# A pairwise bilinear kernel: weights loaded four pairs at a time, inputs one field at a time, outputs stored two pairs at a time

## The chip, the core and the metric

The kernel runs on one core of a Trainium2 chip. The metric is the device time of one execution in microseconds (us); the time before is the median of seven runs.

## What is computed

There are 32 fields of 128 numbers for each of 1024 samples, and one 128 x 128 matrix for each of the 496 pairs (i, j) of fields with i < j. Each pair gives one output block of 1024 x 128, all in float32:

```python
v_i = inputs[:, I_IDX, :]                                # (1024, 496, 128)
v_j = inputs[:, J_IDX, :]
transformed = jnp.einsum('bpd,ped->bpe', v_i, W)         # W: (496, 128, 128)
return transformed * v_j
```

The inputs are 16.8 MB, the weights 32.5 MB and the output 260 MB.

## The kernel before

Everything is laid out transposed: the 128 numbers of a field (or of an output block) lie over the 128 partitions, the 1024 samples along the free dimension. In HBM a field is 128 rows of 4 KB, and two neighbouring fields lie side by side in each partition's row. The weights lie in groups, each partition's part of a group being contiguous, and so do the output blocks.

The pairs are taken with i falling from 30 to 0 and j rising from i + 1 to 31, so the blocks of pairs with equal i grow from 1 pair to 31. A pair is worked on in two halves of 512 samples, called units; unit u is half u % 2 of pair u // 2.

*Numbers.* Only the first 15 pairs (NATIVE) are multiplied in plain float32, by one matmul (L145). For all others, x and the weights are split into a high, a low and a difference part in the format float32r. split_w (L87 to L95) does this for a chunk of four pairs (WC = 4): one operation on ScalarE (L92) and three on GpSimd (L93 to L95). split_x (L100 to L109) does it for half a field in the same way (L106, then L107 to L109). A unit then has two matmuls into a PSUM bank (L148), a scaling of that bank in place by ScalarE (L149), and a third matmul on top of it (L157). VectorE multiplies the bank by x_j and writes it into an output tile (L163).

*Order.* The order is written out by hand in one loop over units. In each step, `first(u)` issues L145, or L148 and L149; `second(u - LAG)` with LAG = 3 issues L157, L163 and, when a tile is full, its store. Splits come from a list sorted by due time. PSUM has eight banks, one unit each.

*Transfers.* All loads of weights (L83) and, but for the first two fields, of x (L74), and all stores (L167, and L165 for the halves of the last two pairs) are issued by one queue, SyncE's (SP), in the order of the program. A load of weights brings WL = 8 pairs in 4 KB rows into one of three buffers, and is issued WLEAD = 2 groups ahead. A load of x brings two fields in 8 KB rows; they stay for the whole run. An output tile holds OG = 1 pair; there are six tiles (L64), and VectorE's first write into a tile (L163) waits until the tile's last store has landed. Each DMA issued also waits until the DMA eight places before it has landed.

The lines that set how much is moved at once:

```python
t = xpool.tile([P, n, BT], F32, tag=f"x{f}", name=f"x_{f}")
w_raw[c] = rpool.tile([P, WL, P], F32, tag="w", name=f"w_{c}")
ots[g] = opool.tile([P, OG, BT], F32, tag="ot", name=f"ot_{g}")
```

Of the kernel before, what the change touches and what calls it, by code (L numbers as in the profile page):

```python
# [1 line left out]

# [4 lines left out]

F32 = mybir.dt.float32
F32R = mybir.dt.float32r
ALU = mybir.AluOpType  # L10

P = 128
NF = 32
NQ = NF * (NF - 1) // 2
BT = 1024
HB = 512
WC = 4
WL = 8
OG = 1
EPS = 2.0**-12  # L20
NATIVE = 5
LAG = 3
WLEAD = 2
XLEAD = 4


def _pairs():

    return [(i, j) for i in range(NF - 2, -1, -1) for j in range(i + 1, NF)]


@with_exitstack
def kernel(
    ctx: ExitStack,
    tc: tile.TileContext,
    xt: bass.AP,
    wt: bass.AP,
    out: bass.AP,
):

    nc = tc.nc
    pairs = _pairs()
    nchunk = NQ // WC

    xpool = ctx.enter_context(tc.tile_pool(name="x", bufs=1))  # L60
    spool = ctx.enter_context(tc.tile_pool(name="xs", bufs=2))
    rpool = ctx.enter_context(tc.tile_pool(name="wr", bufs=3))
    wpool = ctx.enter_context(tc.tile_pool(name="ws", bufs=3))
    opool = ctx.enter_context(tc.tile_pool(name="o", bufs=6))  # L64
    ppool = ctx.enter_context(tc.tile_pool(name="ps", bufs=8, space=bass.MemoryType.PSUM))

    x_sb = {}

    def load_x(f, n=1, pieces=1, eng=None):

        t = xpool.tile([P, n, BT], F32, tag=f"x{f}", name=f"x_{f}")
        s = BT // pieces
        for k in range(pieces):
            (eng or nc.sync).dma_start(out=t[:, :, k * s : (k + 1) * s], in_=xt[:, f : f + n, k * s : (k + 1) * s])  # L74
        for k in range(n):
            x_sb[f + k] = t[:, k, :]

    w_raw = {}

    def load_w(c, splits=(0, WL)):  # L80
        w_raw[c] = rpool.tile([P, WL, P], F32, tag="w", name=f"w_{c}")
        for a, b in zip(splits, splits[1:]):
            nc.sync.dma_start(out=w_raw[c][:, a:b, :], in_=wt[c, :, a:b, :])  # L83

    w_s = {}

    def split_w(c):  # L87

        k = c * WC % WL
        raw = w_raw[c * WC // WL][:, k : k + WC, :].rearrange("p q e -> p (q e)")  # L90
        h, l, d = [wpool.tile([P, WC * P], F32R, tag=t, name=f"{t}_{c}") for t in ("wh", "wl", "wd")]
        nc.scalar.mul(h, raw, 1.0 - 2.0**-13)  # L92
        nc.gpsimd.tensor_tensor(l, raw, h.bitcast(F32), ALU.subtract)  # L93
        nc.gpsimd.tensor_scalar(d, h.bitcast(F32), EPS, 1.0, ALU.mult, ALU.mult)  # L94
        nc.gpsimd.tensor_tensor(d, l.bitcast(F32), d.bitcast(F32), ALU.subtract)  # L95
        w_s[c] = (h, l, d)

    x_s = {}

    def split_x(f, a):  # L100

        if a == 0:
            x_s[f] = [spool.tile([P, BT], F32R, tag=t, name=f"{t}_{f}") for t in ("xh", "xl", "xd")]
        s = slice(a, a + HB)
        h, l, d = [t[:, s] for t in x_s[f]]
        nc.scalar.mul(h, x_sb[f][:, s], 1.0 - 2.0**-13)  # L106
        nc.gpsimd.tensor_tensor(l, x_sb[f][:, s], h.bitcast(F32), ALU.subtract)  # L107
        nc.gpsimd.tensor_scalar(l, l.bitcast(F32), 1.0 / EPS, 1.0, ALU.mult, ALU.mult)  # L108
        nc.gpsimd.tensor_tensor(d, h.bitcast(F32), l.bitcast(F32), ALU.subtract)  # L109

    nq0 = NATIVE * (NATIVE + 1) // 2
    c0 = nq0 // WC
    first_q = {i: q for q, (i, j) in reversed(list(enumerate(pairs)))}

    todo = []
    for c in range(c0, nchunk):
        todo.append(((c - 2) * WC + 1, max(c * WC, nq0), lambda c=c: split_w(c)))
    for i in range(NF - 2 - NATIVE, -1, -1):  # L120
        for a in range(0, BT, HB):
            todo.append((first_q[i + 1] + 1 if i < NF - 3 - NATIVE else 2, first_q[i], lambda i=i, a=a: split_x(i, a)))
    todo.sort(key=lambda t: t[1])

    load_w(0, (0, 1, WL))
    load_x(NF - 2, pieces=2, eng=nc.scalar)
    load_x(NF - 1, pieces=2, eng=nc.scalar)
    load_x(NF - 3)
    load_x(NF - 4)
    load_w(1)  # L130
    load_x(NF - 6, 2)


    ctx.enter_context(tc.manual_schedule())
    po, ots = {}, {}


    def first(u):
        q, h = divmod(u, 2)
        i, c = pairs[q][0], q // WC  # L140
        r = slice(q % WC * P, (q % WC + 1) * P)
        s = slice(h * HB, (h + 1) * HB)
        po[u] = ppool.tile([P, HB], F32, tag="po", name=f"po_{u}")
        if q < nq0:
            nc.tensor.matmul(po[u], w_raw[q // WL][:, q % WL, :], x_sb[i][:, s], start=True, stop=True)  # L145
        else:
            for t in (0, 1):
                nc.tensor.matmul(po[u], w_s[c][t][:, r], x_s[i][t][:, s], start=t == 0, stop=t == 1)  # L148
            nc.scalar.mul(po[u], po[u], 1.0 + EPS)  # L149

    def second(u):
        q, h = divmod(u, 2)
        i, j = pairs[q]
        r = slice(q % WC * P, (q % WC + 1) * P)
        s = slice(h * HB, (h + 1) * HB)
        if q >= nq0:
            nc.tensor.matmul(  # L157
                po[u], w_s[q // WC][2][:, r], x_s[i][2][:, s], start=False, stop=True, skip_group_check=True
            )
        g, k = divmod(q, OG)  # L160
        if k == 0 and h == 0:
            ots[g] = opool.tile([P, OG, BT], F32, tag="ot", name=f"ot_{g}")
        nc.vector.tensor_tensor(ots[g][:, k, s], po.pop(u), x_sb[j][:, s], ALU.mult)  # L163
        if q >= NQ - 2:
            nc.sync.dma_start(out=out[g, :, k, s], in_=ots[g][:, k, s])  # L165
        elif k == OG - 1 and h == 1:
            nc.sync.dma_start(out=out[g], in_=ots[g])  # L167

    for u in range(2 * NQ + LAG):
        q = u // 2  # L170
        if u % (2 * WL) == 0 and (q // WL + WLEAD) * WL < NQ:
            load_w(q // WL + WLEAD)
        if u < 2 * NQ:
            i, j = pairs[q]
            if u % 2 == 0 and j == i + 1 and i % 2 == 0 and 0 <= i - 2 - XLEAD:
                load_x(i - 2 - XLEAD, 2)
            first(u)
        if u >= LAG:
            second(u - LAG)
        if u % 2 == 1:  # L180
            ready = [t for t in todo if t[0] <= q]
            if ready:
                ready[0][2]()
                todo.remove(ready[0])
    assert not todo


# [25 lines left out]
```

## Time and profile before

| | |
|---|---|
| median of 7 runs | 781.07 us (779.4 to 787.55) |
| the profiled execution's own time | 782.89 us |
| its span in the profile | 781.1 us |
| granted TensorE clock, mean | 0.976 |
| read from HBM, written to it | 49.28 MB, 260.05 MB |
| over the span | 396 GB/s |

The span runs from the first to the last instruction that the profile shows. PE is TensorE's matmuls, PEld its weight loads, DVE is VectorE, ACT ScalarE, POOL GpSimd and SP SyncE. A group's line gives the source line, the engine and the operation, the tiles written and read, the number of instructions, the busy time and mean duration of one in ns, then the engine's idle time just before them and what ended most of it. A line of DMA issues gives the tiles, the queue, the count, the size and the median us from issue to landing. A digit in the DMA row is the mean busy share of the 16 DMA engines in a fortieth of the span, in tenths (9 is 90% or more); the DMA packet line counts packets by size, and the queue lines give packets, MB and the time that the packets took as a share of 16 engines' span. The chain of waits lists start, length and what ran.

### The profile page before, as it was taken

How to read it: one execution, taken by the hardware profiler on the slowest of the kernel's cores; microseconds unless marked ns; L12 is line 12 of the kernel's file. 1: busy time of each engine (PE TensorE's matmuls, PEld its weight loads, DVE VectorE, ACT ScalarE, POOL GpSimd, SP SyncE). 2: the span in 40 equal slices, each digit the busy share in tenths (PEclk: the TensorE clock that was granted, in tenths of full speed). 3: DMA queues.
4: the chain of work that ended last, by engine and by line, in shares of the span. 5: the costliest groups of instructions: out<-in, count | busy, mean ns of one | idle time of the engine just before them, and what ended most of it. 6: DMA issues, size and time to landing. Idle time of an engine off the chain costs nothing.

```text
span 781.1 us, 11576 instructions
## 1 busy us (share of the span) xinstructions
PE 715.8 (92%) x2946; PEld 557.9 (71%) x2946; DVE 634.9 (81%) x992; ACT 617.1 (79%) x1136; POOL 550.5 (70%) x523
## 2 busy tenths in 40 slices
PE   7989889898997998998998999899999999999994
PEld 3468668676776876776776877777777777777773
DVE  4678768787896978887896988789888889889886
ACT  1279779797886986987886888788888888888883
POOL 0998998787776885866767586767685767594550
PEclk9999999999998999999999999999999999999998
DMA  9999999999999999999999999999999999999997
GB/s 357 417 377 400 409 388 407 404 397 396 412 400 399 389 392 405 400 387 402 403 392 402 390 403 405 398 400 391 404 403 404 401 400 408 404 401 400 403 414 317
DMA packets 83730, 310.10 MB, mean 397 GB/s; under 512 B 9296, under 2 KB 9424, under 8 KB 81872
## 3 DMA queue, kind: packets, MB, share of 16 engines
q1 hardware_dynamic: 83088, 308.32, 100.4%
q10 hardware_dynamic: 576, 1.05, 0.4%
q8 instruction: 23, 0.38, 0.2%
q14 instruction: 43, 0.35, 0.1%
HBM read 49.28 MB, written 260.05 MB: 396 GB/s over the span
## 4 chain that ended last, share of the span: by engine, by line
DMA 53%; DVE 23%; PE 17%; POOL 3%; issue 1%; SPq 0%; DVEq 0%; ACT 0%; POOLq 0%
DMA out_dram<-ot 51%; DVE ot L163 23%; PE po L148 12%; PE po L157 5%; DMA x<-in_xt_dram 1%; POOL xd L109 1%; POOL xl L107 1%; DMA w<-in_wt_dram 1%; POOL wl L93 0%; POOL xl L108 0%; POOL wd L95 0%; DVEq L163 0%; SPq L83 0%; ACT xh L106 0%; POOL wd L94 0%
## 5 line engine op out<-in xcount | busy, mean ns | idle before, releaser
L163 DVE TENSOR_TENSOR ot<-po,x 128x512 f32<-128x512 f32 x992 | 634.9, 686 | 139.1 <-DMA out_dram<-ot 102.2
L149 ACT ACTIVATE po<-po 128x512 f32<-128x512 f32 x962 | 539.4, 581 | 137.1 <-PE po L148 90.4
L148 PE MATMUL po<-xh,wh 128*128 128x512 f32 x962 | 387.9, 403 | 49.0 <-DVE ot L163 48.9
L148 PE MATMUL po<-xl,wl 128*128 128x512 f32 x962 | 380.7, 396 | 2.2 <-POOL wl L93 1.7
L157 PE MATMUL po<-xd,wd 128*128 128x512 f32 x962 | 379.4, 395 | 0.0
L93 POOL TENSOR_TENSOR wl<-w,wh 128x512 fp32r<-128x512 f32 x121 | 156.2, 1291 | 158.1 <-ACT wh L92 158.1
L148 PEld LDWEIGHTS po<-xh,wh 128*128 128x128 f32 x962 | 183.4, 191 | 114.5 <-DVE ot L163 74.6
L157 PEld LDWEIGHTS po<-xd,wd 128*128 128x128 f32 x962 | 183.9, 191 | 40.3 <-ACT po L149 0.4
L148 PEld LDWEIGHTS po<-xl,wl 128*128 128x128 f32 x962 | 184.0, 191 | 37.7 <-POOL wl L93 2.1
L95 POOL TENSOR_TENSOR wd<-wl,wd 128x512 fp32r<-128x512 f32 x121 | 156.6, 1294 | 10.1
L107 POOL TENSOR_TENSOR xl<-x,xh 128x512 fp32r<-128x512 f32 x52 | 67.2, 1293 | 23.1 <-ACT xh L106 23.1
L94 POOL TENSOR_SCALAR wd<-wh 128x512 fp32r<-128x512 f32 x121 | 75.2, 622 | 10.2
L92 ACT ACTIVATE wh<-w 128x512 fp32r<-128x512 f32 x121 | 75.7, 627 | 0.0
L109 POOL TENSOR_TENSOR xd<-xh,xl 128x512 fp32r<-128x512 f32 x52 | 67.0, 1288 | 4.3
L106 ACT ACTIVATE xh<-x 128x512 fp32r<-128x512 f32 x52 | 32.6, 631 | 13.8 <-DMA x<-in_xt_dram 13.8
L108 POOL TENSOR_SCALAR xl<-xl 128x512 fp32r<-128x512 f32 x52 | 32.3, 622 | 4.6
L145 PE MATMUL po<-x,w 128*128 128x512 f32 x60 | 29.2, 651 | 4.2 <-DMA x<-in_xt_dram 4.2
L145 PEld LDWEIGHTS po<-x,w 128*128 128x128 f32 x60 | 12.1, 207 | 20.5 <-issue 13.8
L106 ACT ACT_TABLE_LOAD x1 | 1.3, 1283 | 2.6 <-issue 2.6
L200 POOL MEMSET const-float32-0.0<- 128x1 f32 x1 | 0.1, 99 | 0.2 <-issue 0.2
L200 POOL MEMSET const-bfloat16-1.0<- 128x1 bf16 x1 | 0.1, 102 | 0.0
L200 POOL MEMSET const-uint8-127<- 128x1 uint8 x1 | 0.1, 102 | 0.0
(1 smaller groups left out, 0.1 us busy)
## 6 DMA issues: line engine op xcount, KB each, us to landing
out_dram<-ot SPq DMA_DIRECT2D x494, 512.0 KB, 7.6
w<-in_wt_dram SPq DMA_DIRECT2D x61, 512.0 KB, 7.2
x<-in_xt_dram SPq DMA_DIRECT2D x14, 1024.0 KB, 10.3
x<-in_xt_dram ACTq DMA_DIRECT2D x4, 256.0 KB, 5.7
x<-in_xt_dram SPq DMA_DIRECT2D x2, 512.0 KB, 6.8
out_dram<-ot SPq DMA_DIRECT2D x4, 256.0 KB, 6.1
w<-in_wt_dram SPq DMA_DIRECT2D x1, 448.0 KB, 4.6
w<-in_wt_dram SPq DMA_DIRECT2D x1, 64.0 KB, 3.1
```

Source lines behind the costliest of these rows:

```text
L92: nc.scalar.mul(h, raw, 1.0 - 2.0**-13)
L93: nc.gpsimd.tensor_tensor(l, raw, h.bitcast(F32), ALU.subtract)
L94: nc.gpsimd.tensor_scalar(d, h.bitcast(F32), EPS, 1.0, ALU.mult, ALU.mult)
L95: nc.gpsimd.tensor_tensor(d, l.bitcast(F32), d.bitcast(F32), ALU.subtract)
L106: nc.scalar.mul(h, x_sb[f][:, s], 1.0 - 2.0**-13)
L107: nc.gpsimd.tensor_tensor(l, x_sb[f][:, s], h.bitcast(F32), ALU.subtract)
L109: nc.gpsimd.tensor_tensor(d, h.bitcast(F32), l.bitcast(F32), ALU.subtract)
L145: nc.tensor.matmul(po[u], w_raw[q // WL][:, q % WL, :], x_sb[i][:, s], start=True, stop=True)
L148: nc.tensor.matmul(po[u], w_s[c][t][:, r], x_s[i][t][:, s], start=t == 0, stop=t == 1)
L149: nc.scalar.mul(po[u], po[u], 1.0 + EPS)
L157: nc.tensor.matmul(po[u], w_s[q // WC][2][:, r], x_s[i][2][:, s], start=False, stop=True, skip_group_check=True)
L163: nc.vector.tensor_tensor(ots[g][:, k, s], po.pop(u), x_sb[j][:, s], ALU.mult)
```

## The change

WL goes from 8 to 4: a load of weights brings four pairs, in 2 KB rows instead of 4 KB, into one of five buffers instead of three, and is issued four groups ahead instead of two, so still 16 pairs. OG goes from 1 to 2: an output tile holds two pairs, a store writes 1 MB in 8 KB rows, and there are three tiles instead of six, with the same memory in all. The layout of the output and of the weights in HBM follows OG and WL. A load of x brings one field in 4 KB rows, at the start of each block of pairs with equal i, instead of two fields at every second block. Ahead of the loop, fields 27 and 26 are loaded one by one, and two more groups of weights. SP then issues 247 stores of 1 MB, 125 loads of weights and 30 loads of x, and the four stores of halves at the end as before. The order of the compute instructions stays the same on each engine.

```diff
-WL = 8
-OG = 1
+WL = 4
+OG = 2
 ...
-WLEAD = 2
-XLEAD = 4
+WLEAD = 4
+XLEAD = 3
 ...
-    rpool = ctx.enter_context(tc.tile_pool(name="wr", bufs=3))
+    rpool = ctx.enter_context(tc.tile_pool(name="wr", bufs=5))
 ...
-    opool = ctx.enter_context(tc.tile_pool(name="o", bufs=6))
+    opool = ctx.enter_context(tc.tile_pool(name="o", bufs=3))
 ...
     load_w(1)
-    load_x(NF - 6, 2)
+    for f in range(NF - 5, NF - 4 - XLEAD, -1):
+        load_x(f)
+    load_w(2)
+    load_w(3)
 ...
-            if u % 2 == 0 and j == i + 1 and i % 2 == 0 and 0 <= i - 2 - XLEAD:
-                load_x(i - 2 - XLEAD, 2)
+            if u % 2 == 0 and j == i + 1 and 0 <= i - 2 - XLEAD:
+                load_x(i - 2 - XLEAD)
```

## Prediction

> **What bounds the kernel now.** I read the page first: the engines' shares, the DMA rows, then the releasers. Next come the waits of VectorE (DVE) and the chain of work in a late stretch.
>
> ```profile
> PE 715.8 (92%) x2946; PEld 557.9 (71%) x2946; DVE 634.9 (81%) x992; ACT 617.1 (79%) x1136; POOL 550.5 (70%) x523
> DMA  9999999999999999999999999999999999999997
> DMA packets 83730, 310.10 MB, mean 397 GB/s; under 512 B 9296, under 2 KB 9424, under 8 KB 81872
> q1 hardware_dynamic: 83088, 308.32, 100.4%
> L163 DVE TENSOR_TENSOR ot<-po,x 128x512 f32<-128x512 f32 x992 | 634.9, 686 | 139.1 <-DMA out_dram<-ot 102.2
> L148 PE MATMUL po<-xh,wh 128*128 128x512 f32 x962 | 387.9, 403 | 49.0 <-DVE ot L163 48.9
> out_dram<-ot SPq DMA_DIRECT2D x494, 512.0 KB, 7.6
> w<-in_wt_dram SPq DMA_DIRECT2D x61, 512.0 KB, 7.2
> x<-in_xt_dram SPq DMA_DIRECT2D x14, 1024.0 KB, 10.3
> ```
>
> No compute engine is full: PE has most, and 48.9 us of its idle time is blamed on DVE, whose own 139.1 us of idle is mostly (102.2) waiting for a store to give an output tile back. The DMA engines are at nine tenths or more in every slice but the last, and one queue alone accounts for 100.4% of sixteen engines. So the bound is DMA time. Next, what a tile does, from the chain of waits:
>
> ```profile
> 606.70 3.88 DVE ot L163 x6
> 610.58 0.02 issue
> 610.60 7.64 DMA out_dram<-ot
> ...
> 634.15 7.42 DMA out_dram<-ot
> 641.57 0.03 issue
> 641.60 0.05 DVEq L163
> 641.65 0.04 issue
> 641.69 0.70 DVE ot L163
> ```
>
> A store issues 0.02 us after DVE's last write; 7.4 to 7.6 us later it lands; 0.12 us after that DVE starts (641.57 to 641.69). DVE's pace in a row is 3.88/6 = 0.647 us an operation.
>
> **What a packet costs.** In the trace's packet records the median durations on q1 are 84 ns (2 KB rows), 159 (4 KB), 309 (8 KB, only loads of x) and 9 (the 4-byte completion): 9 ns plus 75 ns per 2 KB. At the very end, where one DMA engine works alone, starts lie 80 ns apart for 2 KB, 155 for 4 KB and 6 for a completion, so some 4 ns of each overlap. I take 305 for 8 KB, an estimate (309 - 4). A DMA puts 8 rows and one completion on each of 16 engines: 512 KB in 4 KB rows 8 x 155 + 6 = 1.246 us, 1 MB in 8 KB rows 2.446, 256 KB in 2 KB rows 0.646.
>
> Against the whole of before: 494 stores, 62 weight loads' worth and x come to about 735 us per engine; DMA is active from 3.3 us to the end, some 775. The other 40 are stalls and instruction fetches. Packets last longer than their medians by 7.7 us (8 KB) and 24 us (4 KB) per engine.
>
> **The change part by part.**
>
> *Stores, 494 of 512 KB to 247 of 1 MB (8 KB rows):* 247 x (2 x 1.246 - 2.446) = -11.4 us. *Weights, 62 loads in 4 KB rows to 124 in 2 KB rows:* 62 x (2 x 0.646 - 1.246) = +2.9. *x, 14 loads of two fields to 28 of one, 8 KB to 4 KB rows:* 14 x 0.046 = +0.6. Together -7.9 us. Every microsecond is on the path, as the DMA engines have no gap. Upper bound of the gain: the full 9 ns per removed packet, (83088 - 58464) x 9 / 16 = -13.9 us. Lower bound: none; the last landings in the trace come 1.25 us apart for 512 KB in 4 KB rows and 0.63 apart for 256 KB in 2 KB rows, the same per byte. Below nothing it goes only if 8 KB stores stall (rival 2). I take -7.9, between.
>
> Here rules speak against the row. The Trainium skill ("DMA: Bandwidth & Descriptors", Specifications) has line rate from 512 B up, so 2, 4 and 8 KB rows would cost the same and this part is worth 0; by 80, 155 and 305 ns it is -7.9. The same page (Rules for kernel authors) asks for 1 MiB or more per DMA, and gives (Anatomy of one DMA) some 2 us fixed for each, there for DMAs issued from GpSimd: 62 more weight loads would be +124 us and 247 fewer stores -494, if DMAs ran one at a time. In this trace neither shows: behind a queued store a 512 KB weight load lands 1.24 us after it, so the fixed time is hidden by the queue. I follow the rows.
>
> *Stalls of x.* The 8 KB rows of x last 378 ns in the mean for a median of 309. Behind a queued store a 1 MB load of x lands 3.6 us later, where two stores take 2.6. The start of the run has x in 4 KB rows: excess 2 ns a packet, against 33 for the 8 KB rows right after. The 4 KB rows of weights have about 13 (stretches with a weight load have 7.3 a packet, stretches of stores alone 4.7, and a third of the packets are the load's: 4.7 + 3 x 2.6). If x takes 13 per 4 KB, 1792 x (69 - 26)/16 = -4.8 us. Bounds: 0 if the stall goes by bytes, +7.7 if by packet, -7.7 if it goes. I take -4.8, nearest to the 4 KB rows of x and w. *Stalls of weights:* 2 KB rows of x at the start have 0.6 ns excess; if by packet, 7900 more x 13/16 = +6.4; if by byte 0. I take +1.
>
> *Tiles, six of one pair to three of two.* The bytes are the same; the grain is not. Before: fill 2 x 0.647, start and issue 0.14, empty-queue latency 1.2 (the fastest first landing of a 512 KB store is 2.45 us after issue, less its 1.25), transfer 1.3: 3.9 us out of six periods of 1.55 = 9.3. So 5.4 us of queue wait are forecast, and 7.6 - 2.5 = 5.1 are there. After: fill 2.59, 0.14, 1.2, transfer 2.53: 6.46 us out of three periods of 3.1 = 9.3, leaving 2.8 us. Positive, so the slowest DMA engine still has work. But engines differ: in the trace the first of 16 completions of a store comes at 4.6 us (median) and the last at 7.6, a spread of 3. With 2.8 us of cover the fastest engines will sometimes run dry. They catch nothing up later, so I charge +2; bounds 0 (a dry fast engine isn't the bound) and +17 (rival 2).
>
> *Waits on SP.* A store now waits for four DVE writes instead of two. Queued behind it on SP are the next weight load or x; they lead by nine pairs (14 us) for weights, as before, and four or more fields for x. No one needs them that early. Each DMA waits on the one eight before it; with at most three stores out that one has landed. The first split of x needs one field at about 15.5 us instead of two at 17.7, since less is loaded ahead; DMA is saturated there anyway, so 0. Compute instructions stay the same in number and order; PE at 0.68 us a unit (0.45 + 0.23 in the chain) needs 2.72 us per two pairs, DVE 2.59: both below the 3.1 that the DMA engines need. Fewer SP instructions are worth 0.
>
> Sum: -7.9 - 4.8 + 1 + 2 = -9.7 us on the profiled execution's 782.9 us (1.8 around its 781.1 span): 773.2. That execution lies 1.8 above the median of 781.07, so 771.4 against the median.
>
> **The rivals.**
> 1. *Rows don't matter* (0.2): the wire gain is nil as the last landings suggest, and the x stall goes by bytes: 781.1 + 1 + 2 = 784, or 778 if half of both gains comes (-6.4); 781 in the middle. For it: equal landings per byte at the end. Against: the packet starts.
> 2. *Three tiles are too few* (0.3, slower). Each load of x delays some DMA engine more than the mean: a 1 MB load cost the slowest 1.0 us and the mean engine 0.55. With 5.1 us of wait the others absorb that; with 2.8 against a spread of 3.0 the loss is paid each time, and every new stall of the slowest stops all 16. Worked out: 28 loads x up to 0.6 us = +17, on top of -7.9 + 1: 791. It decides from 11.7 us of added dry time (7.9 + 4.8 - 1), that is 0.047 us per two-pair tile. Stalls of 8 KB stores would do the same: 6 ns a packet over 31616 packets / 16 engines is 11.9 us. No store of 8 KB rows is in the trace; instruction fetches of 8 KB last 309, without stalls, which speaks against it.
> 3. *Everything at its best* (part of the forecast's own side): -13.9 - 7.7 gives 760.
>
> **How the numbers follow.** The forecast case (771.4, own range 764 to 777) has 0.5, rival 1 (777 to 784) 0.2, rival 2 (785 to 800) 0.3. A measurement here tells some 0.5%, 3.9 us, from no change: faster 0.5, same 0.18, slower 0.32, a little of rival 1 spilling over. The range reaches from 763 to 793, leaving out the end of rival 2 and the best case.
>
> **What would show it.** Right: q1 with 58464 packets and 8 KB stores at a median of 309; DMA rows still at 9; store landing near 6.5 us for 1 MB (9.2 less 2.59 and 0.14); DVE's waits for stores still first; mean of x packets near 170 ns. Wrong: 8 KB packets well above 309 in the mean; DMA share falling under nine tenths in middle slices with fewer than 16 packets in flight (rival 2); PE or ACT becoming the releaser of most DVE idle; more GB/s without a shorter span can't be, as the bytes are fixed.

## The result and the profile after

The changed kernel takes 773.94 us (median of 12 runs, 769.92 to 776.26), the kernel before 781.17 us (31 runs): a ratio of 0.9902, 95% interval 0.9884 to 0.992, or -7.7 us. The forecast was -9.7 us (771.4). The profiled execution took 772.85 us against 782.89.

These are the lines of the page after that answer to those shown of before:

```profile
PE 721.7 (94%) x2946; PEld 552.8 (72%) x2946; DVE 617.2 (80%) x992; ACT 620.0 (80%) x1136; POOL 550.8 (71%) x523
DMA  9899999999999999999999999999999999999999
DMA packets 59102, 310.04 MB, mean 402 GB/s; under 512 B 6561, under 2 KB 6817, under 8 KB 27425
q1 hardware_dynamic: 58464, 308.31, 99.4%
L166 DVE TENSOR_TENSOR ot<-po,x 128x512 f32<-128x512 f32 x992 | 617.2, 684 | 147.9 <-DMA out_dram<-ot 92.5
L151 PE MATMUL po<-xh,wh 128*128 128x512 f32 x962 | 390.7, 406 | 37.0 <-DVE ot L166 34.8
out_dram<-ot SPq DMA_DIRECT2D x247, 1024.0 KB, 6.2
w<-in_wt_dram SPq DMA_DIRECT2D x123, 256.0 KB, 5.9
x<-in_xt_dram SPq DMA_DIRECT2D x30, 512.0 KB, 7.3
```

The bytes are the same, the packets some 30% fewer, and the queue still fills its engines to 99.4%. The DMA row has an 8 in its second slice, where before it had a 9. A 1 MB store lands 6.2 us after its issue (6.5 was forecast). DVE's main wait is still for a store.

The packet records tell more, as us for each of the 16 engines. "Stalls" is what all packets of q1 last beyond 9 ns and 75 ns per 2 KB; "dry" is the time with fewer than 16 packets in flight between 45 and 750 us, counted as missing packets over 16.

| | before | after |
|---|---|---|
| packets of q1 | 83088 | 58464 |
| stalls, us | 31.7 | 28.0 |
| of them 8 KB packets | 7.7 (x) | 23.0 (stores) |
| dry, us | 3.0 | 4.7 |
| first to last completion of a store, median us | 3.05 | 1.48 |

With the prediction's 5 ns for a packet, 24624 packets fewer are worth -7.7 us; with -3.7 for stalls and +1.7 for dry time that makes -9.7, and the two profiled executions differ by -10.0. So the sum looks as forecast. But the experiments show that its term for the tiles was far too small, and that two others were off the other way and made up for it.

### The profile page after: what moved, and what is told of

Its sections match the earlier page's. It is cut to its first block, busy times and chain, and to the rows that moved or that the text cites. A ratio compares the mean times of both kernels' runs of the same rounds, so it can differ in the third digit from the quotient of the medians.

```text
span 771.1 us, 10983 instructions
## 1 busy us (share of the span) xinstructions
PE 721.7 (94%) x2946; PEld 552.8 (72%) x2946; DVE 617.2 (80%) x992; ACT 620.0 (80%) x1136; POOL 550.8 (71%) x523
## 3 DMA queue, kind: packets, MB, share of 16 engines
q1 hardware_dynamic: 58464, 308.31, 99.4%
## 4 chain that ended last, share of the span: by engine, by line
DMA 42%; PE 33%; DVE 22%; issue 1%; DVEq 0%; SPq 0%; ACTq 0%
DMA out_dram<-ot 41%; DVE ot L166 22%; PE po L151 22%; PE po L160 10%; DMA x<-in_xt_dram 1%; DVEq L166 0%; ACTq L74 0%; SPq L74 0%; SPq L83 0%; DVEq L209 0%; SPq L170 0%
## 5 line engine op out<-in xcount | busy, mean ns | idle before, releaser
L166 DVE TENSOR_TENSOR ot<-po,x 128x512 f32<-128x512 f32 x992 | 617.2, 684 | 147.9 <-DMA out_dram<-ot 92.5
L94 POOL TENSOR_SCALAR wd<-wh 128x512 fp32r<-128x512 f32 x121 | 75.2, 621 | 10.2
```

## The experiments

All ratios are to runs of the kernel before on the same chip; 0.001 is 0.78 us.

**Each half alone.** Stores alone (e1):

```diff
-OG = 1
+OG = 2
 ...
-    opool = ctx.enter_context(tc.tile_pool(name="o", bufs=6))
+    opool = ctx.enter_context(tc.tile_pool(name="o", bufs=3))
```

> The change's stores alone: two pairs per store in 8 KB rows, three tiles; the loads stay as before (eight pairs of weights, two fields). Theory (the row size of the stores is the gain): -11.4 us of DMA time for the stores, +2 to +4 for DMA engines that run dry: 772 to 774 us, as fast as the whole change. Rival (the finer loads bring it, three tiles need them): 781 or more, since the 1 MB loads of x now meet three tiles only.

Measured: 803.57 us, 1.0269 (1.0225 to 1.0312). The rival, and far beyond its 781. Loads alone (e2, the changed kernel with OG = 1 and six tiles again):

```diff
-OG = 2
+OG = 1
 ...
-    opool = ctx.enter_context(tc.tile_pool(name="o", bufs=3))
+    opool = ctx.enter_context(tc.tile_pool(name="o", bufs=6))
```

> The change's loads alone: four pairs of weights in 2 KB rows, one field of x in 4 KB rows; stores stay at one pair in 4 KB rows from six tiles. Theory: +2.9 us (weights) + 0.6 (x) of packet time, -4 for the stalls of 8 KB rows of x that go: 780 to 782 us, no change. Rival (finer loads are the gain): 774.

Measured: 778.21 us, 0.9959 (0.9945 to 0.9972). So the halves bring +2.7% and -0.4% alone, and -1.0% together: the stores pay only with the finer loads. Two lines of the waits of e1 (who waited <- for whom: us, times, longest) show where:

```profile
DVE ot L163 <- DMA out_dram<-ot: 129.3, 69, 4.9
PE po L148 <- DVE ot L163: 64.0, 49, 4.0
```

DVE waits 129 us for tiles, where before it was 102, and PE 64 us for DVE instead of 49. In e1's packet records the dry time is 20.7 us (3.0 before) and the stalls are 47.6 (31.7).

**Row size alone (e3).** The output's layout in HBM gives the 1 MB stores 4 KB rows; DMAs, tiles and waits stay:

```diff
-            nc.sync.dma_start(out=out[g], in_=ots[g])
+            nc.sync.dma_start(out=out[g].rearrange("k p b -> p k b"), in_=ots[g])
 ...
-    args.append(nc.dram_tensor("out_0_dram", (NQ // OG, P, OG, BT), F32, kind="ExternalOutput").ap())
+    args.append(nc.dram_tensor("out_0_dram", (NQ // OG, OG, P, BT), F32, kind="ExternalOutput").ap())
```

> The changed kernel with one thing undone: each 1 MB store still is one DMA from a two-pair tile, but the output's layout in HBM makes its rows 4 KB, 256 of them, instead of 8 KB, 128 of them. Same DMAs, same tiles, same waits. Theory (a packet costs some 5 ns beside its bytes): 247 x (16 x 155 + 6 - 2446) ns = +9.9 us on 773.9: 784. Rival (rows from 512 B up run at line rate, so row size is nothing, and the gain is from fewer or finer DMAs): 774.

Measured: 787.84 us, 1.009 (1.0059 to 1.012), which is 14.7 us (+-2.8) above the changed kernel. Rows count, and by more than forecast: 9.9 us of packets at 5 ns, and in the records 2.9 us more stalls and 2.4 us more dry time, 15.2 together. The same in the kernel before (e9), each store with 2 KB rows instead of 4 KB:

```diff
-            nc.sync.dma_start(out=out[g], in_=ots[g])
+            nc.sync.dma_start(out=out[g].rearrange("h p s -> p h s"), in_=ots[g][:, 0, :].rearrange("p (h s) -> p h s", h=2))
```

> The kernel before with one thing changed: each 512 KB store, still one DMA per pair from six tiles, writes 2 KB rows (256 of them) instead of 4 KB (128), by the output's layout in HBM. Theory (a packet costs 5 to 9 ns beside its bytes, and DMA is the bound): 494 x 8 more packets per engine, +19.8 us at 5 ns, +35.6 us at 9 ns: 801 to 817. Rival (rows from 512 B up run at line rate): 781.

Measured: 813.02 us, 1.0408 (1.0381 to 1.0435). From its page, the rates by slice and the queue:

```profile
GB/s 357 404 374 375 393 385 392 382 385 385 389 375 387 379 372 398 382 377 397 382 380 384 391 386 371 384 399 382 388 383 378 387 391 380 385 389 375 394 394 316
q1 hardware_dynamic: 146320, 308.32, 102.0%
```

The queue is as full as before, with some 385 GB/s instead of 400. 32 us for 494 x 8 packets more per engine is 8.1 ns each; e3's 14.7 us for 247 x 8 is 7.4. These prices have the stalls and dry time in them that come along: in e9, 19.8 us are packets at 5 ns, 7.3 stalls and 2.3 dry time.

**The length of a load.** The changed kernel with eight pairs of weights a load (e4):

```diff
-WL = 4
+WL = 8
 ...
-WLEAD = 4
+WLEAD = 2
 ...
-    rpool = ctx.enter_context(tc.tile_pool(name="wr", bufs=5))
+    rpool = ctx.enter_context(tc.tile_pool(name="wr", bufs=3))
 ...
-    load_w(2)
-    load_w(3)
```

> The changed kernel with the weights as before: eight pairs in 4 KB rows, three buffers, two groups ahead. Theory: -2.9 us of packet time, 771. Rival (finer weight loads help three tiles keep DMA fed): 776 or more, as a 512 KB load in the queue holds up a tile twice as long.

Measured: 790.51 us, 1.0125 (1.0085 to 1.0164), 17.4 us above the changed kernel: the rival, and more than it asked (776 or more). Dry time is 13.8 us, 9.1 more than in the changed kernel; stalls are 44.3 us, 16.3 more, so dry time alone is not the loss. With 2 KB rows in the same 512 KB load (e6, by the layout of the weights in HBM; the rest of the edit is e4's):

```diff
-                nc.sync.dma_start(out=w_raw[c][:, a:b, :], in_=wt[c, :, a:b, :])
+                nc.sync.dma_start(out=o.rearrange("p (h q) e -> p h q e", h=2), in_=wt[c].rearrange("h p q e -> p h q e"))
 ...
```

> The changed kernel with loads of eight pairs of weights (512 KB, one DMA, two groups ahead), which ran 790.5 us with 4 KB rows, now with the weights laid out in HBM so that the rows are 2 KB. Theory (the length of the load in the queue hurts three tiles): 790 to 793, as with 4 KB rows. Rival (4 KB rows of weights stall among stores, 18 ns a packet against 1 for 2 KB rows): 778 to 782.

Measured: 790.53 us, 1.0115 (1.0099 to 1.0132): the same as with 4 KB rows. It is the length of the load, not its rows. With x in pairs again in the changed kernel (e5; what is loaded ahead of the loop goes back too):

```diff
-            if u % 2 == 0 and j == i + 1 and 0 <= i - 2 - XLEAD:
-                load_x(i - 2 - XLEAD)
+            if u % 2 == 0 and j == i + 1 and i % 2 == 0 and 0 <= i - 2 - XLEAD:
+                load_x(i - 2 - XLEAD, 2)
 ...
```

> The changed kernel with x as before: two fields a load in 8 KB rows, at every second block. Theory (with three tiles, a long load in the queue makes VectorE wait for tiles, TensorE stops with full banks and cannot catch up, and the DMA engines run dry afterwards): 14 long loads of 2.5 us and more each cost some 0.5 us, and their 8 KB rows stall by 4 us more: 782, half the damage of the 61 loads of 512 KB of weights. Rival (it is the 4 KB rows of the weights that hurt, not the length of a load): 778, the stalls of x alone.

Measured: 779.8 us, 0.9988 (0.9971 to 1.0004), 6.7 us (+-1.9) above the changed kernel, between the two figures (some 8 and 4 above), so this run does not tell them apart. With e4's 17.4 it comes near the 28.7 us that e1, which has both long loads, lies above the changed kernel. In the kernel before, x in single fields alone (e10, the same edit backwards):

> The kernel before with the loads of x alone changed, one field in 4 KB rows; weights, stores and six tiles stay. Theory (8 KB rows of x stall, 4 KB rows less so): +0.6 - 4: 777 to 778, all of the 3.3 us that the finer loads gained together. Rival (the finer weights gave it): 781.

Measured: 778.24 us, 0.9963 (0.9946 to 0.998), -2.9 us: as the theory has it, and next to nothing is left for the finer weights with six tiles (0.9959 with both).

**How a long load runs DMA dry.** e4's DVE in time, in one place (start, length, instructions, idle before and what ended it), and then the windows there (us, then busy us and count for PE, PEld, DVE, ACT and POOL, the granted clock, the DMA share and GB/s):

```profile
180.21 4.88 DVE L164 TENSOR_TENSOR ot<-po,x 128x512 f32<-128x512 f32 x8 [1.26 <-DMA out_dram<-ot]
189.32 4.40 DVE L164 TENSOR_TENSOR ot<-po,x 128x512 f32<-128x512 f32 x7 [4.24 <-DMA out_dram<-ot]
193.89 6.17 DVE L164 TENSOR_TENSOR ot<-po,x 128x512 f32<-128x512 f32 x9 [0.17 <-PE po L158]
```

```profile
188.00:190.00 2.00, 0.00 (x0) 0.00 (x0) 0.68 (x2) 0.00 (x0) 1.96 (x2) 0.95 1.01 426
190.00:191.00 1.00, 0.93 (x2) 0.83 (x3) 1.00 (x3) 0.00 (x0) 0.87 (x2) 0.50 1.02 434
191.00:192.00 1.00, 1.00 (x4) 0.71 (x3) 1.00 (x3) 0.58 (x1) 1.00 (x1) 0.50 0.30 123
192.00:193.00 1.00, 1.00 (x4) 0.81 (x3) 1.00 (x2) 0.40 (x1) 0.03 (x1) 0.50 0.45 188
193.00:194.00 1.00, 1.00 (x5) 0.77 (x5) 0.83 (x3) 0.53 (x2) 0.00 (x0) 0.89 1.07 426
```

DVE waits 4.24 us for a tile; PE, its eight banks full, stands still (0.00 from 188 to 190) and restarts at half the granted clock (0.50). For two microseconds little is left for the DMA engines: their share falls to 0.30 and 0.45. In the kernel before the same happens at 240 us, after a wait of DVE of 4.97 us, and the DMA engines do not notice:

```profile
240.00:241.00 1.00, 0.00 (x0) 0.00 (x0) 0.66 (x2) 0.00 (x0) 0.96 (x1) 0.50 1.05 430
241.00:245.00 4.00, 3.91 (x9) 3.14 (x10) 3.88 (x7) 1.26 (x3) 1.91 (x2) 0.50 1.02 417
```

At these two places the stores from six tiles lasted through the whole restart, and those from three tiles of twice the size did not. Over whole runs, e2 and e3 differ in this alone (six tiles of one pair, three of two, all rows of the stores 4 KB), and their dry time is 2.8 and 7.1 us.

With three tiles, what follows a dry stretch costs about as much again. Packets that start 1 to 4 us after a moment with fewer than 14 in flight carry 18.8 us of e4's stalls, at 52 to 61 ns a packet against 9 later on. In e3 they carry 7.9 us, in the changed kernel 6.6, in e2 1.1, in the kernel before 2.6. Why they last longer stays open.

The test is to speed the catching up: e4 without the third matmul of each unit (e8; its low-order term is left out):

```diff
-        if q >= nq0:
-            nc.tensor.matmul(
-                po[u], w_s[q // WC][2][:, r], x_s[i][2][:, s], start=False, stop=True, skip_group_check=True
-            )
```

> The kernel with eight pairs of weights per load, two-pair tiles and single fields (790.5 us), leaving out the third matmul of each unit (its low-order correction), so that TensorE needs 0.45 us a unit instead of 0.68; all transfers stay. Theory (TensorE's slow catching up after a wait is what lets DMA run dry): 772 to 778. Rival (three tiles and long loads suffice on their own): 788 to 791.

Measured: 777.37 us, 0.9943 (0.9922 to 0.9965), 14 us less than e4 with the same transfers; its q1 is at 99.1%, its dry time 7.2 us and its stalls 34.1, against 13.8 and 44.3 in e4. DVE even waits longer for tiles (117.0 us, e4 99.8), yet the DMA engines run dry less. So with long loads and three tiles the loss hangs on the time that TensorE needs for a unit. No run leaves the third matmul out of a kernel with short loads, so how much of the 14 us would come there too is not shown.

```profile
PE 630.1 (81%) x1984; PEld 327.7 (42%) x1984; DVE 612.2 (79%) x992; ACT 608.4 (79%) x1136; POOL 547.8 (71%) x523
q1 hardware_dynamic: 49536, 308.30, 99.1%
DVE ot L160 <- DMA out_dram<-ot: 117.0, 85, 3.7
```

e4's line for the same wait:

```profile
DVE ot L164 <- DMA out_dram<-ot: 99.8, 68, 5.0
```

**Two tiles (e7).**

```diff
-    opool = ctx.enter_context(tc.tile_pool(name="o", bufs=3))
+    opool = ctx.enter_context(tc.tile_pool(name="o", bufs=2))
```

> The changed kernel with two output tiles of two pairs instead of three. Theory (the loop of a tile is what the prediction added up: 2.59 us filling, 0.14 start and issue, 1.2 empty-queue latency, 2.5 transfer, 6.4 to 6.5 together, half the loads in between): two tiles give at least 6.46/2 = 3.23 us for each of 248 tiles, 801 us, and with the loads that fall into the loop (some 0.3 us of each tile's 0.65 for weights and x) up to 870. Rival (tiles are not the limit, DMA engines are, whatever the tiles): 774 to 780.

Measured: 935.25 us, 1.1971 (1.1949 to 1.1993), beyond the 870 of the theory too. The chain's shares over the whole span, and a piece of it in the middle, in order of time:

```profile
DMA 57%; DVE 30%; PE 10%; issue 1%; POOL 1%; DVEq 1%; SPq 0%; POOLq 0%
```

```profile
505.64 4.48 DMA out_dram<-ot
...
510.24 0.70 DVE ot L166
...
510.99 0.73 PE po L151 x2
...
513.33 2.50 DVE ot L166 x4
...
515.84 6.16 DMA out_dram<-ot
```

935/248 = 3.77 us a tile, against 3.23 in the sum: the loop of two tiles takes 7.54 us where 6.46 were added up. By the shares of the chain some 4.3 us of it are DMA, against 3.73 for latency and transfer, and some 3.0 DVE and PE, against 2.59 for the filling. So the sum is a floor for two reasons: a store still lands later than an empty queue would have it (4.48 us in the piece, 6.16 once), and a fill after a wait is not always at DVE's pace. In the piece DVE writes once, waits from 510.9 to 513.3 while the chain runs over PE, and then writes four times in 2.50 us.

**Going further.** x laid out by fields in HBM, the fields from 23 down in two halves two pairs apart, field 25 loaded early (e11):

```diff
 ...
+    load_x(NF - 2 - NATIVE)
 ...
+                if j == i + 1:
+                    load_x(f, 0, HB if j + 2 < NF else BT)
+                elif j == i + 3:
+                    load_x(f, HB, BT)
 ...
```

> The changed kernel, with x laid out field by field in HBM, each field loaded in two halves of 256 KB three pairs apart, and field 25 (which the first split needs) loaded ahead of 27 and 26. Theory (shorter loads keep three tiles from running dry, and the 2.5 us in which DMA ran dry near the start go): -2 to -6 on 773.9: 768 to 772. Rival (the loads are fine enough by now, and only the tiles' bytes count): 774.

Measured: 771.43 us, 0.9877 (0.9851 to 0.9904). Inside the theory's range and the fastest of all, but its interval overlaps the changed kernel's. The dry stretch near the start (2.6 us between 20 and 45 us after the change) is gone, and no half-clock stretch of TensorE is left between 45 and 750 us. On top of it, tiles of 2, 2, 2 and 1 pairs; to make room, weights go into four buffers and are issued three groups ahead (e12):

```diff
-    opool = ctx.enter_context(tc.tile_pool(name="o", bufs=3))
+    opool = ctx.enter_context(tc.tile_pool(name="o", bufs=1))
 ...
-            ots[g] = opool.tile([P, OG, BT], F32, tag="ot", name=f"ot_{g}")
+            ots[g] = opool.tile([P, n, BT], F32, tag=f"ot{g % 4}", name=f"ot_{g}")
```

> The kernel of the run before this one (fields in halves, 771.4 us) with output tiles of 2, 2, 2 and 1 pairs in turn, four tiles of 28 KB instead of three of 24 KB; every fourth store writes 4 KB rows, and weights are issued three groups ahead into four buffers to make room. Theory (dry stretches of the DMA engines are what three tiles still cost): the 71 stores with 4 KB rows cost 71 x 8 x 4 ns = +2 us, and the remaining dry time of some 5 us goes: 767 to 770. Rival (what is left is packets and stalls, so tiles buy nothing more): 773.

Measured: 772.3 us, 0.9904 (0.9874 to 0.9934): the rival, nearly. Its dry time is 5.0 us, e11's 4.8; a fourth, smaller tile did not lessen what dry time is left.

## Why the prediction was right, and where it was not

The bound was read rightly (DMA time, with no slack), and so was the sign: -9.7 forecast, -7.7 measured. That the size came so near is in part luck: the tiles cost 8 us more than forecast, and weights and rows together 7.5 us less. Point by point, with the runs' ratios turned into microseconds (the steps lead from the kernel before over e10, e2 and e3 to the changed one, so they add up to the whole by construction):

| step | forecast | measured |
|---|---|---|
| x: packets and stalls | +0.6 - 4.8 | -2.9 +-1.3 (e10) |
| weights: packets and stalls | +2.9 + 1 | -0.3 +-1.7 (e2 less e10) |
| three tiles of two pairs, rows kept at 4 KB | +2 | +10.2 +-2.6 (e3 less e2) |
| rows of the stores 4 to 8 KB | -11.4 | -14.7 +-2.8 (after less e3) |
| sum | -9.7 | -7.7 |

The packet records split such differences further: packets at 5 ns, stalls and dry time, beside the difference of the two profiled executions, in us.

| | packets | stalls | dry | sum | executions |
|---|---|---|---|---|---|
| x (e10 less before) | +0.6 | -6.4 | +0.2 | -5.6 | -5.9 |
| tiles (e3 less e2) | -1.2 | +9.2 | +4.4 | +12.4 | +11.1 |
| rows (after less e3) | -9.9 | -2.9 | -2.4 | -15.2 | -15.7 |
| long weights (e4 less after) | -2.8 | +16.3 | +9.1 | +22.7 | +20.9 |
| no third matmul (e8 less e4) | 0.0 | -10.2 | -6.6 | -16.8 | -17.7 |

The sums come within 2 us of the measured differences, so the 5 ns a packet fit, and in the tiles and the long loads the stalls outweigh the dry time.

- *x* was right: single fields in 4 KB rows cost more packets and save more stalls. Whether the stall goes with the rows or with the length of the load is not separated, since both changed.
- *Weights*: neither the +1 for stalls nor the +2.9 for packets showed in the time. From e10 to e2 the records have the packets (+2.8 at 5 ns), and stalls that fall by 3.7 us (25.3 to 21.6) where a rise was forecast.
- *Tiles* is the term that failed: "They catch nothing up later, so I charge +2." The landing was forecast well (6.2 us against 6.5), so the queue wait was too, and the spread of the engines shrank from 3.05 to 1.48 us. The cost lay in DMA engines that run dry and in what follows: e3 has 4.4 us more dry time than e2, and 6.8 us more stalls on packets that start 1 to 4 us after such a stretch. The likely reason is the production after a wait. The prediction noted that PE's 2.72 us and DVE's 2.59 us per two pairs are "both below the 3.1" and stopped there; by the same figures PE has 12% of slack, so it needs some eight times a lost stretch to make up for it (an estimate). With long loads e8 shows that TensorE's pace decides; with short loads, where the +10.2 was measured, this is argued and not tested. Rival 2 had the right place (three tiles) and came near the size, +17, with coarse loads: e4 has it. Its mechanism, engines of unequal speed, is not the main one there: with the same transfers e8 is 14 us faster.
- *Rows* were undersized: the packets' own price of 5 ns was right, but in the full queue more stalls and more dry time come with the smaller packets (2.9 and 2.4 us). With them a packet costs 7.4 ns, nearer to the prediction's upper bound of 9. The Trainium skill's line rate from 512 B up ("DMA: Bandwidth & Descriptors", Specifications), set against the row there, does not hold here: rows of 2 KB instead of 4 cost 32 us (e9). 8 KB stores stall by 11.7 ns a packet, two 4 KB packets by 9.4 before (twice the 4.7 that the prediction has), so what rival 2 feared of them is some 4.5 us and not 11.9. The line that spoke against it there was misread: instruction fetches of 8 KB have a median of 309 ns, but a mean of 340, so they do stall.
- *Start*: "DMA is saturated there anyway, so 0" was wrong by a little. The DMA engines ran dry for 2.6 us between 20 and 45 us. It is not the smaller lead of x: with single fields but eight pairs of weights a load (e4, e10) it is 0.0 us there, with four pairs it is 1.3 (e2), 2.2 (e3) and 1.8 (e5).

What the whole hangs on, and the prediction did not see: the finer loads are not a cost beside the gain but its condition. With 512 KB of weights the same stores end at 790 us.

It stays open why packets stall after a dry stretch and why more time goes with small rows, and how much of e5's 6.7 us is the length of the loads and how much their rows.

## What to carry to other kernels

When a buffer's bytes are dealt into fewer and larger pieces, count not only the queue wait that is left but the time the producer needs to catch up after the longest transfer in that queue; cut that transfer first. In a kernel bound by DMA, rows are worth measuring even from 2 to 4 to 8 KB: a packet had a price of 7 to 8 ns here, 5 of them its own. Test the halves of such a change both alone and together: one of them looked 2.7% bad alone and brings 4.5 of the 7.7 us once the other is there.

## What was not expected of the hardware

After a stop of TensorE of 1.9 to 4.2 us its granted clock was 0.5 for 3.41 us (at times twice that): eight such stretches between 45 and 750 us in the kernel before, six after, one in e2 and in e10. The Trainium skill ("TensorE: Matmul & The Clock Gate", What's actually happening) gives a window of 3413 ns for it, which the length of the stretches matches; all but one of the stops before them were shorter than that. With six tiles it cost DMA next to nothing (0.2 us of dry time within 3 us of such stretches before), with three and long loads 6.3 of e4's 13.8 us of dry time lie near them. The half clock alone does not run the DMA engines dry: e8 has sixteen such stretches, with 3.5 us of dry time within 3 us of them.
